# Ranks of messages pinned in three parts, and the first part of x loaded and normed first, in a two-layer graph kernel

## The chip, the cores and the metric

The kernel runs on one core of one Trainium2 chip. The metric is the device time of one execution in microseconds (us): the median of several runs, and beside it one execution that was taken with the hardware profiler, from which all durations below come. The engines are named as the profile names them: PE (matmuls), PEld (its weight loads), DVE (VectorE), ACT (ScalarE), POOL (GpSimd) and SP, which here only issues DMAs and loads registers. "DVE L807" is an instruction of VectorE that line 807 of the kernel before has issued.

## The reference

Two graph layers over 6250 nodes with 128 features and 106250 edges (100000 random ones in both directions, and a loop at each node), sorted by destination.

```python
edge_index = jnp.stack([src, dst])
h = jnp.maximum(_layernorm(x, axis=-1), 0.0)
x = x + layer0(h, edge_index, edge_type, ...)       # attention, 4 relations, 8 heads
h = jnp.maximum(_layernorm(x, axis=-1), 0.0)
x = x + layer1(h, edge_attr, src, dst, ...)         # messages both ways along each edge
```

Layer 0 projects the nodes once for each of four relations, takes a softmax of leaky logits over the edges that enter a node, for each relation and head, sums the weighted rows of the sources, and mixes the relations with a second small attention. Layer 1 computes `leaky_relu([nf[src], nf[dst], ef] @ We1) @ We2` for each edge in both directions, sums it at the node where it ends, and updates the node. So in layer 1 each edge gives one message to its destination and another to its source; the destinations are sorted, the sources are not.

## The kernel before

**Preparation** (lines 198 to 436). The nodes are cut into 50 units of 126 (`NU`, two blocks of 63, one in each half of the partitions). The weights come by ACT's DMA queue. The edge lists `src`, `dst`, the types `et` and the shifted `nxt` come by SP's queue as tiles of 128 x 832; then all of `x`, in five parts of ten units, each part as four DMAs (lines 242 to 252; the first two parts by ACT's queue, behind the weights, the rest by SP's). From the lists VectorE makes small tables that go to DRAM: `e2` (table row and destination of each edge), `turnd` (where a run of equal destinations begins or goes on, six writes), `lacks` (for each relation, the edges not of it, four writes from tiles `ne` of two buffers) and `dtyp` (lines 278 to 297), all on SP's queue. It also finds where each block's edges start (lines 301 to 345, into `st0`). SP then reads those starts into registers, ten at a time (line 165), and issues for each of the 100 blocks a load of its `e2` rows into `ct` (lines 350 to 358). Ten functions `columns` (line 364) turn `ct` into index columns `xi` and `dloc`; they stand in front of the last ten units.

The loop over units (lines 376 to 404) norms ten units at a time (`layernorm_relu`, line 141, into `h_sb` of two buffers), transposes a unit (PE L384), copies it (ACT, `hT`), multiplies it by the weights (PE L391, L394), copies the result to `row` (DVE L392) and `so` (ACT L398), both of three buffers, and stores them: `own` by ACT's queue (L400), the gather table `xt` by POOL's (L403). The DMAs of SP's and ACT's queues signal through eight semaphores that are handed out in turn over both queues; a DMA waits until the one that had its semaphore before has landed. The order of instructions on each engine comes from a scheduler, except where `tc.keep_in_program_order` pins an instruction; an engine then executes its instructions strictly in that order.

**Layer 0** (lines 441 to 891) goes in 25 steps `s` of four blocks, each of nine tiles `i` of 4 x 128 edges. POOL gathers the rows of `xt`, four gathers a tile (line 85, called in `gather0`), 17 tiles ahead, into 18 buffers `xg`. Each step, VectorE, ScalarE and PE do the messages of step `s` (line 604) and beside them the softmax of step `s + 1`: `logits` (line 530), four running scans in both directions (L571, L574, L581, L584) with a piece before an exponential (L577) and one behind a logarithm (L588), and `turn` (line 592), which leaves the weights `pw`. A dictionary `todo` says at which tile, and at which half of it, each of these pieces is issued: (i, 0) in the middle of the tile's four blocks, (i, 1) behind them. The nodes of step `s - 1` are finished in the same step (line 646).

**Ranks.** Layer 1 writes each message for a source to a place of its own. The place is a rank: how many edges before this one, in the same fifth of the partitions, go to a source of the same unit. Units are taken in 25 pairs. For each pair `count` (line 738) counts them, one VectorE instruction; `counted` (line 745) turns the counts into starting places in step 4; `rank` (line 802) then takes three instructions on the whole list of 128 x 832, for each pair:

```python
stt(own_, skey, float(g), sunit, op0=ALU.is_equal, op1=ALU.mult)
scan(place, own_, own_, base1[:, g:g + 1], op0=ALU.add, op1=ALU.max)
nc.vector.copy_predicated(plc, own_.bitcast(I32), place)
```

`own_` and `place` have one buffer each, and all operands lie in SBUF (`sunit` is bf16). `rank_at` (line 825) issues them behind tile 0 of steps 4, 5, ..., and also behind tile 5 of odd steps. They are not pinned. Behind the last pair `ranked` (line 810) makes the places whole, eight more instructions and one store, `plcd`, that layer 1 reads.

**Layer 1** (lines 945 to 1147) again gathers (900 times) and also scatters (900 times) with POOL.

Of the kernel before, what the change touches and what calls it, by code (L numbers as in the profile page):

```python
# [9 lines left out]
F32 = mybir.dt.float32  # L10
BF16 = mybir.dt.bfloat16
I32 = mybir.dt.int32
U8 = mybir.dt.uint8
AF = mybir.ActivationFunctionType
ALU = mybir.AluOpType
# [6 lines left out]
P = 128  # L22
# [4 lines left out]
R = 4  # L27
H, D = 8, 16
C = H * D
# [5 lines left out]
J = 832  # L35
JL = E - (P - 1) * J
JE = P * J
# [5 lines left out]
GB = 63  # L43
DB = 2 * GB
NU = -(-N // DB)
# [6 lines left out]
NS = NBK // Q  # L52
XR = C + H
SX = 2 * C + 2 * H
NEAR = 2.0 ** 100
# [3 lines left out]
NCS = 4  # L59
# [30 lines left out]
def kernel(ctx: ExitStack, tc: tile.TileContext, x, src, dst, ef, et, w_rel, a_src, a_dst,  # L90
# [10 lines left out]
    nc = tc.nc  # L101
# [96 lines left out]
    with ExitStack() as prep:  # L198
# [4 lines left out]

        wall = cpool.tile([P, R * XR + R * H + C + 2 * H], F32, name="wall")
# [24 lines left out]
        ints = {}  # L229
# [11 lines left out]

        x_sb = cpool.tile([P, NU, C], F32, name="x_sb")
        for u0 in range(0, NU, 10):
            nc.gpsimd.memset(x_sb[:, u0:u0 + 10, :], 0.0)
            for q in range(2):
                n0 = u0 * DB + q * GB
                k = 10 if u0 + 10 < NU else 9
                xq = x[u0 * DB:(u0 + k) * DB, :].rearrange("(u q r) c -> q r u c", q=2, r=GB)[q]
                for r0, r1 in ((0, 48), (48, GB)):
                    (nc.scalar if u0 < 20 else nc.sync).dma_start(x_sb[q * 64 + r0:q * 64 + r1, u0:u0 + k, :], xq[r0:r1])  # L250
        for h, n in halves(NU - 1):
            nc.sync.dma_start(x_sb[h, NU - 1, :], x[n, :])

# [30 lines left out]
        dn = cpool.tile([P, 2, J], BF16, name="dn")  # L284
        tt(dn[:, 1, :], ints["dst"], nxt, op=ALU.is_equal)
        ts_(dn[:, 0, :], dn[:, 1, :], -1.0, NEAR, op0=ALU.add, op1=ALU.mult)
        for k in range(2):
            nc.sync.dma_start(turnd[k, 1:JE + 1].rearrange("(p j) -> p j", j=J), dn[:, k, :])
            for o, w in ((0, 1), (JE + 1, 7)):
                nc.sync.dma_start(turnd[k:k + 1, o:o + w], dn[0:1, k, 0:w])  # L290
        for r in range(R):
            ne = wpool.tile([P, J], BF16, name="ne")
            ts_(ne, ints["et"], float(r), None, op0=ALU.not_equal)
            nc.sync.dma_start(lacks[r].rearrange("(p j) -> p j", j=J), ne)
        dty = cpool.tile([P, J], F32, name="dty")
        stt(dty, dstf, float(R), ints["et"], op0=ALU.mult, op1=ALU.add)
        nc.sync.dma_start(dtyp[0].rearrange("(p j) -> p j", j=J), dty)

# [61 lines left out]

        first = cpool.tile([P, NBK, TB], F32, name="first")
# [14 lines left out]
        for u in range(NU):  # L376
            if u >= NU - NBK // CG:
                columns(u - NU + NBK // CG)
            if u % 10 == 0:
                h_sb = wpool.tile([P, 10, C], F32, name="h_sb")  # L380
                sq = wpool.tile([P, 10, C], F32, name="sq", bufs=1)
                layernorm_relu(wpool, h_sb, x_sb[:, u:u + 10, :], sq)
            tp = pp.tile([P, P], F32, name="tp")
            nc.tensor.transpose(tp, h_sb[:, u % 10, :], ident)  # L384
            hT = wpool.tile([P, P], F32, name="hT")
            nc.scalar.copy(hT, tp)
            row = wpool.tile([P, R * XR], F32, name="row", bufs=3)
# [9 lines left out]
            so = wpool.tile([P, SX], F32, name="so", bufs=3)  # L397
# [43 lines left out]
    with ExitStack() as s1_:  # L441
# [360 lines left out]
        def rank(g):  # L802

            own_ = wp.tile([P, J], F32, name="own_", bufs=1)
            stt(own_, skey, float(g), sunit, op0=ALU.is_equal, op1=ALU.mult)
            place = wp.tile([P, J], F32, name="place", bufs=1)
            scan(place, own_, own_, base1[:, g:g + 1], op0=ALU.add, op1=ALU.max)  # L807
            nc.vector.copy_predicated(plc, own_.bitcast(I32), place)
# [16 lines left out]
        rank_at = [(s, i) for s in range(NCS, NS) for i in ((0, 5) if s % 2 else (0,))]  # L825
# [24 lines left out]
        for s in range(NS):  # L850
# [5 lines left out]
            if more:  # L856
                work(s + 1)
                for at, f in zip(((2, 0), (3, 1), (4, 0), (4, 1), (5, 0), (5, 1), (6, 0), (7, 0), (8, 0)), soft(s + 1)):
                    todo[at] = f
                for c in range(3):  # L860
                    todo[c, 1] = lambda c=c: logits(s + 1, c)
                gts.append(wp.tile([P, 2, R + 1], F32, name="gt", bufs=3))
            for i in range(TB):
                n = s * TB + i
                if n + LA0 < NS * TB:
                    gather0(n + LA0)
                messages(s, i, acc, turns_, todo.get((i, 0), lambda: None))
                todo.get((i, 1), lambda: None)()
                if more and i <= R:
                    tallies(s + 1, i, gts[s + 1])  # L870

                g = NC0 + s * TB + i
                if g < NU // 2:
                    count(g, True)
                if (s, i) == (NCS, 0):
                    counted()
                if (s, i) in rank_at[:NU // 2]:
                    rank(rank_at.index((s, i)))
                    if rank_at.index((s, i)) == NU // 2 - 1:
                        ranked()  # L880
                if i == 5 and s + 2 < NS:
                    loads(s + 2)
# [840 lines left out]
```

## Time and profile before

| | us |
|---|---|
| median of 3 runs (4106.76 to 4119.22) | 4111.01 |
| the profiled execution | 4104.87 |
| its span, first to last instruction | 4103.1 |
| busy: PE / DVE / ACT / POOL | 3053 / 2739 / 1545 / 2892 |
| first transposes of a unit (PE L384) | 42.9 |
| last load of `ct` issued (SP L356) | 146.4 |
| first gather (POOL L85) | 158.7 |
| last gather of layer 0 | 1402.3 |
| end of the last GELU of layer 0 (ACT L631) | 1468.2 |

A step of layer 0 is measured here from the end of its predecessor's eighth GELU (L631) to the end of its own. The steps, in us:

| step | 1 | 2 | 3 | 4 | 5 | 6 | 7 | 8 | 9 | 10 | 11 | 12 |
|---|---|---|---|---|---|---|---|---|---|---|---|---|
| length | 47.8 | 47.6 | 51.6 | 48.6 | 59.5 | 54.1 | 54.8 | 53.5 | 55.8 | 51.6 | 52.2 | 47.3 |
| in ranks (DVE) | 1.0 | 0 | 0 | 7.1 | 11.7 | 12.5 | 15.3 | 14.2 | 16.1 | 13.7 | 12.5 | 3.1 |

Steps 13 to 23 take 46.4 to 49.3 each and hold no rank. The three instructions of a rank take 1.02, 1.95 and 1.09; the first scan of a rank starts at 447.1, the last copy at 835.2.

How to read the profile's lines: a group line has the source line, engine, operation, output and input tiles, the count, then the busy time and the mean of one in ns, then the idle time of the engine just before, with what ended it. A timeline line has the start, the duration, engine, line and operation, and in brackets the idle time before it. A line of the windows view has the window, its length, and for PE, PEld, DVE, ACT and POOL the busy time with the number of instructions; then the granted clock of PE, the DMA share and GB/s. A line of the wait table has who waited for whom, the total in us, the times, and the longest. A busy sum of an engine does not say that it is the bottleneck: that is read from what ends the waits in a stage.

### The profile page before, as it was taken

Reading aid. Unit: us, or ns where it says so; the run is one execution under the profiler, and the core shown is the slowest. Engines: PE = TensorE matmul, PEld = TensorE weight load, DVE = VectorE, ACT = ScalarE, POOL = GpSimd, SP = SyncE. Lnnn points to the kernel's source line nnn. Section 1 sums busy time; section 2 is a strip of 40 time slices with the busy share of each in tenths; the row PEclk is TensorE's granted clock in tenths of the full one; section 3 lists DMA queues with packets and bytes.
Section 4 is the critical chain, followed back from the end, with each engine's and each line's share of the span. In section 5 each row is a group of like instructions: output and inputs, shape, how many; then the busy total and the mean of one; then the engine's idle time right before and its main releaser. Section 6 shows DMA issues by size and latency. Waiting matters only on the chain. (4 is left out here: it accounts for less than half of the span.)

```text
span 4103.1 us, 43438 instructions
## 1 busy us (share of the span) xinstructions
PE 3053.0 (74%) x11258; PEld 1729.4 (42%) x11258; DVE 2738.6 (67%) x5139; ACT 1545.1 (38%) x2990; POOL 2892.2 (70%) x2887
## 2 busy tenths in 40 slices
PE   4468877778887756666678877778768777688888
PEld 3346555555555532222234342334324333244455
DVE  7467888887777745555466665666657666577755
ACT  3256655566666622222223333222222322222211
POOL 5777787777777527777777777777777777777600
PEclk9669978899999978888899898999989998899999
DMA  7544444455555356666587886888868878588754
GB/s 193 160 101 122 115 114 115 116 123 121 122 129 127 92 135 186 178 178 182 164 252 236 254 249 183 246 245 242 248 198 259 246 234 248 174 260 272 228 167 140
DMA packets 414557, 754.19 MB, mean 184 GB/s; under 512 B 182846, under 2 KB 249380, under 8 KB 414300
## 3 DMA queue, kind: packets, MB, share of 16 engines
q0 software_dynamic: 148800, 430.91, 35.8%
q1 hardware_dynamic: 234314, 290.32, 27.2%
q10 hardware_dynamic: 31186, 30.10, 2.6%
q8 instruction: 92, 1.51, 0.2%
q14 instruction: 165, 1.35, 0.1%
HBM read 586.37 MB, written 164.69 MB: 183 GB/s over the span
## 5 line engine op out<-in xcount | busy, mean ns | idle before, releaser
L85 POOL DMA_INDIRECT xg<-xt,xi x900 | 970.8, 1079 | 274.4 <-issue 224.6
L1113 POOL DMA_INDIRECT m2d<-s,placei x900 | 913.1, 1015 | 294.6 <-issue 211.4
L85 POOL DMA_INDIRECT ag<-abtab,srci x900 | 907.7, 1009 | 294.6 <-issue 205.4
L1105 PE MATMUL z<-rhs,lt 128*128 128x512 f32 x1800 | 1032.5, 701 | 0.6 <-ACT lt L1069 0.6
L1109 DVE TENSOR_TENSOR s<-s,z 128x1024 f32<-128x1024 f32 x450 | 548.1, 1220 | 549.1 <-ACT z L1108 547.7
L1125 PE MATMUL sums<-s,oh 128*64 128x256 f32 x1800 | 335.2, 455 | 491.3 <-DVE s L1109 490.6
L1107 DVE TENSOR_TENSOR s<-z,ag 128x1024 f32<-128x1024 f32 x450 | 549.8, 1222 | 198.8 <-PE z L1105 154.3
L617 PE MATMUL acc<-oh,msg 128*128 128x256 f32 x1800 | 534.3, 435 | 174.2 <-DVE oh L616 168.9
L1108 ACT ACTIVATE z<-s 128x1024 f32<-128x1024 f32 x450 | 461.1, 1025 | 414.8 <-DVE s L1107 413.5
L1105 PEld LDWEIGHTS z<-rhs,lt 128*128 128x128 f32 x1800 | 352.5, 216 | 447.9 <-issue 441.0
L1016 PE MATMUL sums<-mt,ohw 128*128 128x256 f32 x2024 | 523.3, 392 | 8.7 <-DVE ohw L1015 8.7
L1110 ACT COPY s<-srcf 128x2 f32<-128x2 f32 x450 | 86.7, 193 | 1175.8 <-DMA m2d<-s,placei 1159.9
L617 PEld LDWEIGHTS acc<-oh,msg 128*128 128x128 f32 x1800 | 365.2, 216 | 279.7 <-DVE oh L616 210.3
L1016 PEld LDWEIGHTS sums<-mt,ohw 128*128 128x128 f32 x2024 | 389.3, 198 | 198.0 <-issue 128.5
L1125 PEld LDWEIGHTS sums<-s,oh 128*64 128x64 f32 x1800 | 98.6, 149 | 727.6 <-DVE s L1109 579.4
L616 DVE TENSOR_SCALAR oh<-iota,key 128x256 f32<-128x256 f32 x900 | 307.6, 363 | 144.0 <-PE acc L617 136.0
L624 ACT ACTIVATE junk<-dt,nthr 128x1152 bf16<-128x1152 f32 x250 | 312.9, 1252 | 0.2
L1015 DVE TENSOR_SCALAR ohw<-col,at 128x128 f32<-128x128 f32 x1012 | 250.1, 302 | 15.6 <-PE sums L1016 7.9
L1069 ACT COPY lt<-tp 64x384 f32<-64x384 f32 x300 | 141.7, 472 | 108.0 <-PE tp L1065 55.8
L1065 PE MATMUL tp<-ident,fe 128*128 128x128 f32 x450 | 83.6, 292 | 125.5 <-ACT lt L1069 95.6
L607 DVE TENSOR_TENSOR msg<-xg,pw 128x512 f32<-128x512 f32 x225 | 150.8, 684 | 14.6 <-ACT pw L602 14.4
L542 ACT COPY es<-xg 128x128 f32<-128x128 f32 x225 | 62.1, 297 | 221.1 <-DMA xg<-xt,xi 175.8
(417 smaller groups left out, 3227.3 us busy)
## 6 DMA issues: line engine op xcount, KB each, us to landing
mt<-m2d SPq DMA_DIRECT2D x156, 514.0 KB
db<-in_dst_dram SPq DMA_DIRECT2D x200, 288.0 KB
mt<-m2d SPq DMA_DIRECT2D x53, 642.5 KB
dt<-dtyp SPq DMA_DIRECT2D x100, 288.0 KB
fe<-in_edge_attr_dram SPq DMA_DIRECT2D x100, 288.0 KB
mt<-m2d SPq DMA_DIRECT2D x41, 385.5 KB
xg<-xt,xi POOLq DMA_INDIRECT x900
ag<-abtab,srci POOLq DMA_INDIRECT x900
```

What stands on the lines that cost most here:

```text
L85: nc.gpsimd.indirect_dma_start(out=o, out_offset=None, in_=table, in_offset=bass.IndirectOffsetOnAxis(ap=idx.bitcast(I32), axis=0))
L616: ts_(oh.rearrange("p t n -> p (t n)"), iota, key[:, k:k + 1], None, op0=ALU.is_equal)
L617: nc.tensor.matmul(acc[q // 2][:, :, q % 2, :], msg[:, q, :], oh, start=(i == 0 and q % 2 == 0), stop=(i == TB - 1), skip_group_check=True)
L624: nc.scalar.activation(junk, lanes[s]["dt"][v], AF.Sign, bias=nthr[:, u, t:t + 1], accum_out=g[:, v, t:t + 1])
L1015: ts_(oh, col, at[:, i:i + 1], None, op0=ALU.is_equal)
L1016: nc.tensor.matmul(sums, oh, mt[:, i, 0:HID], start=(i == 0), stop=(i == n - 1))
L1105: nc.tensor.matmul(z[:, q, :], lt[q][:, i * P:(i + 1) * P], rhs[(2 * u + q) % 4], start=True, stop=True)
L1107: tt(s[:, :, 0:2 * HID], z, ags.pop(n), op=ALU.add)
L1108: nc.scalar.mul(z, s[:, :, 0:2 * HID], 0.01)
L1109: tt(s[:, :, 0:2 * HID], s[:, :, 0:2 * HID], z, op=ALU.max)
L1113: st = nc.gpsimd.indirect_dma_start(out=m2d, out_offset=bass.IndirectOffsetOnAxis(ap=placei[:, k:k + 1], axis=0), in_=s[:, q, HID:HID + MW ...
L1125: nc.tensor.matmul(sums[q * 64:(q + 1) * 64, :], oh[:, q * TB + i, :], s[:, q, 0:HID], start=(i == 0), stop=(i == TB - 1))
```

## The change

Two things are changed.

First, the ranks. `rank` now returns its three instructions, and each is issued and pinned at its own half tile: the first pair of a step at (0, 0), (1, 0) and (2, 1), the second pair, in odd steps alone, at (7, 1), (8, 0) and (8, 1). The pairs go to the same steps in the program as before, 4 to 20; now their place on VectorE is theirs.

Second, the preparation. The loads of the first ten units of `x` are issued ahead of most weights on ACT's queue; the first four units are normed by themselves, early, the next six in front of the first unit, and each following ten seven units ahead, in a ring of 20. `row` and `so` get six buffers, `hT` three. The making of `turnd`, `lacks` and `dtyp` and their eleven writes move behind the loads of `ct`, where the writes are pinned on SP's queue.

```diff
+        x_sb = cpool.tile([P, NU, C], F32, name="x_sb")
+        def load_x(u0, queue):
+            nc.gpsimd.memset(x_sb[:, u0:u0 + 10, :], 0.0)
...
+                    queue.dma_start(x_sb[q * 64 + r0:q * 64 + r1, u0:u0 + k, :], xq[r0:r1])
+
+        def norm(u0, n):
+            sq = wpool.tile([P, 10, C], F32, name="sq", bufs=1)
+            layernorm_relu(wpool, h_sb[:, u0 % 20:u0 % 20 + n, :], x_sb[:, u0:u0 + n, :], sq[:, 0:n, :])
+
+        h_sb = cpool.tile([P, 20, C], F32, name="h_sb")
+        load_x(0, nc.scalar)
...
-        x_sb = cpool.tile([P, NU, C], F32, name="x_sb")
-        for u0 in range(0, NU, 10):
...
+        load_x(10, nc.scalar)
+        for u0 in range(20, NU, 10):
+            load_x(u0, nc.sync)
...
+        norm(0, 4)
...
-        dn = cpool.tile([P, 2, J], BF16, name="dn")
...
-        nc.sync.dma_start(dtyp[0].rearrange("(p j) -> p j", j=J), dty)
...
             cts.append(ct)
...
+        dn = cpool.tile([P, 2, J], BF16, name="dn")
...
+        c = nc.sync.dma_start(dtyp[0].rearrange("(p j) -> p j", j=J), dty)
+        tc.keep_in_program_order(c)
...
-            if u % 10 == 0:
-                h_sb = wpool.tile([P, 10, C], F32, name="h_sb")
-                sq = wpool.tile([P, 10, C], F32, name="sq", bufs=1)
-                layernorm_relu(wpool, h_sb, x_sb[:, u:u + 10, :], sq)
+            if u == 0:
+                norm(4, 6)
+            if u % 10 == 3 and u + 7 < NU:
+                norm(u + 7, 10)
...
-            hT = wpool.tile([P, P], F32, name="hT")
+            hT = wpool.tile([P, P], F32, name="hT", bufs=3)
...
-            row = wpool.tile([P, R * XR], F32, name="row", bufs=3)
+            row = wpool.tile([P, R * XR], F32, name="row", bufs=6)
...
-            so = wpool.tile([P, SX], F32, name="so", bufs=3)
+            so = wpool.tile([P, SX], F32, name="so", bufs=6)
...
-            stt(own_, skey, float(g), sunit, op0=ALU.is_equal, op1=ALU.mult)
             place = wp.tile([P, J], F32, name="place", bufs=1)
-            scan(place, own_, own_, base1[:, g:g + 1], op0=ALU.add, op1=ALU.max)
-            nc.vector.copy_predicated(plc, own_.bitcast(I32), place)
+            return [lambda: stt(own_, skey, float(g), sunit, op0=ALU.is_equal, op1=ALU.mult),
+                    lambda: scan(place, own_, own_, base1[:, g:g + 1], op0=ALU.add, op1=ALU.max),
+                    lambda: nc.vector.copy_predicated(plc, own_.bitcast(I32), place)]
...
-        rank_at = [(s, i) for s in range(NCS, NS) for i in ((0, 5) if s % 2 else (0,))]
+        rank_at = [(s, at) for s in range(NCS, NS) for at in (((0, 0), (1, 0), (2, 1)), ((7, 1), (8, 0), (8, 1)))[:1 + s % 2]]
...
+            pairs = [(g, at) for g, (t, at) in enumerate(rank_at[:NU // 2]) if t == s]
+            ranks = {}
+            def half(i, h):
+                f = todo.get((i, h))
+                if f:
+                    f()
+                for g, at in pairs:
+                    if (i, h) == at[0]:
+                        ranks[g] = rank(g)
+                    if (i, h) in at:
+                        tc.keep_in_program_order(ranks[g][at.index((i, h))]())
+                    if (i, h) == at[2] and g == NU // 2 - 1:
+                        ranked()
...
-                messages(s, i, acc, turns_, todo.get((i, 0), lambda: None))
-                todo.get((i, 1), lambda: None)()
+                messages(s, i, acc, turns_, lambda: half(i, 0))
+                half(i, 1)
```

## The prediction

> **What bounds the kernel now.** I read the page first (busy shares, the costliest groups), then the windows view cut at the steps of layer 0, then the timelines of GpSimd and VectorE beside each other, then the timelines and the wait table of the first 160 us. The chain of waits ends in the last store and tells nothing here.
>
> The page's costliest group is the gather of layer 0: 900 instructions on GpSimd, one behind the other, with only issue gaps between them.
>
> ```profile
> L85 POOL DMA_INDIRECT xg<-xt,xi x900 | 970.8, 1079 | 274.4 <-issue 224.6
> ```
>
> An undisturbed gather takes 0.95 us and the next one starts 0.30 us later, so 36 gathers, one step, need 45.2 us. A step (from the last GELU of L631 of one step to that of the next) takes 46.5 to 49 us where no rank runs. Layer 0 is bound by GpSimd. The windows view over six steps with 20 ranks and their closing instructions (steps 6 to 11) and six steps without (13 to 18); columns are PE, PEld, DVE, ACT, POOL:
>
> ```profile
> 550.60:872.70 322.10, 243.12 (x1045) 169.30 (x1044) 286.01 (x555) 189.73 (x356) 256.24 (x217) 0.85 0.48 113
> 920.00:1205.20 285.20, 234.00 (x1040) 164.80 (x1038) 218.47 (x494) 188.56 (x355) 219.68 (x216) 0.92 0.53 126
> ```
>
> The reader is to see that the first six steps are 36.9 us longer and that POOL is busy 36.5 us longer with the same gathers. VectorE still idles 36 us there. So ranks cost time through longer gathers, not through a full VectorE: 36.9 / 20 = 1.85 us a pair. The timelines show how:
>
> ```profile
> 657.56 1.95 DVE L807 TENSOR_TENSOR_SCAN place<-own__6835,base 128x832 f32<-128x832 f32 x1
> 657.65 2.62 POOL L85 DMA_INDIRECT xg<-xt,xi  x1 [0.30 <-issue]
> ...
> 987.78 2.56 DVE L574 TENSOR_TENSOR_SCAN a<-km,f 128x1152 f32<-128x1152 f32 x1
> 988.06 0.95 POOL L85 DMA_INDIRECT xg<-xt,xi  x1 [0.30 <-DVE f L571]
> ```
>
> A gather that starts 0.09 us into a rank scan (both inputs in SBUF) ends 0.76 us after that scan; one that starts in a softmax scan (one input in PSUM) is not touched. A gather that started before the rank instruction is not touched either: the hold is decided at the gather's start.
>
> The other part is the preparation, until the first gather:
>
> ```profile
> 42.92 0.69 PE L384 MATMUL tp<-ident,h_sb 128*128 128x128 f32 x2 [6.92 <-DVE h_sb L156]
> ...
> 62.77 83.93 SPq L356 DMA_DIRECT2D ct<-e  x100
> ...
> 149.50 0.29 DVE L367 CAST ctf<-ct 90x256 f32<-90x256 int32 x1 [4.78 <-DMA abtab<-zr]
> ...
> 158.66 1.40 POOL L85 DMA_INDIRECT xg<-xt,xi  x1 [0.46 <-DMA t<-turnd]
> ```
>
> The first transposes wait for the norm until 42.9; the 50 units follow; the hundred column loads on SP run in step with the units (they share eight completion semaphores with the `own` stores, and the wait table has SP waiting for those stores) and end at 146.7; the last columns and the last unit follow them, then the gathers. As gathers run without a pause from here to 1402, what is won here is won at the end.
>
> **Part 1, the ranks.** Nothing is removed: 25 times 1.02 + 1.95 + 1.09 us (rows of L805, L807, L808) stay, 101 us. They move from steps 4 to 11, up to four pairs a step, to steps 4 to 20, one or two a step. VectorE is busy 36.4 us of 47.6 in a step without ranks; with 4.1 or 8.1 more it still idles 3 us or more, so VectorE itself does not become the bound. What matters is the price at GpSimd. From both sides, by the rows: a gather under the first part took 0.95 to 2.11 us (0 to 1.16 more), one under the scan 1.43 to 2.75 (0.5 to 1.8), one under the copy 0.95 to 1.98 (0 to 1.0): 0.5 to 4.0 us a pair, 12 to 100 us for 25, against 46 now. For parts that stand alone and meet the gathers at any phase I work out the middle: a start in the first L - 0.19 us of a part waits for the rest, starts come every 1.26 us, so 0.83²/2/1.26 = 0.27 and 0.90²/2/1.26 = 0.32 for the two short parts, and 1.95 - 0.63 - 0.19 = 1.13 for the scan. 1.72 a pair, 43 for 25. I take this, which is nearest to the measured 1.85: -3 us. The relief that fewer ranks in a step seem to offer is paid out again over more steps. What waits behind a pinned part on VectorE: the second pair's first part stands in front of the sum of logarithms (old L588), so the weights come 1 us later in eight steps. From a step's last gather to its weights `pw` 40 us pass (877.1 to 917.7 for step 13); the first gather that needs a tile so freed starts at 925.8, which leaves some 5 us after the first `msg`. So that 1 us is hidden; without this cover it would cost 8 us in all.
>
> The Trainium skill, page "SBUF — State Buffer", section "Who interferes with whom", says that a VectorE instruction with two SBUF inputs contends with a GpSimd instruction that reads SBUF, and that the one that comes second blocks fully; it speaks against this change, since a lock is not eased by spreading its holders. The same section infers that descriptor generation needs only the write interface, by which two-input instructions would not hold these gathers at all and the ranks would cost them nothing before or after; the 2.62 us above says otherwise.
>
> **Part 2, the first part of x and its norm.** The four loads of units 0 to 9 go ahead of the small weights on ACT's queue, and a norm of four units is made first. In the changed program's order VectorE runs, from the arrival of `src` (7 to 9.5 us), priced by the distance of starts in the timeline of before: source units and `dstf` 8.1; reduces and subtract of the first units, at 0.4 and 0.6 of 1.46 each, 2.1; weight scores 3.8; `node`, `nthr` 0.8; `e2t`, `ends`, `holds`, `fall`, `dn`, one `ne` 5.9; `less`, count, second `ne` and the rest of the norm 3.7. 24.4 in all, so the first units are normed at about 33 instead of 42.9: 10 us earlier. The x loads have some 7 us until their reduce; the weights, now four issues later, have 8 us.
>
> **Part 3, pace of the units.** First to 47th `own` store: 47.35 to 141.52, 2.05 us a unit. Deeper `row`, `so` and `hT` take these waits away, and norms asked for seven units ahead those for `h_sb`:
>
> ```profile
> ACT so L398 <- DMA own<-so: 24.5, 28, 2.1
> DVE row L392 <- DMA xt<-row: 12.5, 11, 2.0
> ```
>
> They overlap, so not 37 us go. Next late are: VectorE at first (14 `row` copies at 0.68 and 20.6 us of norms and preparation stand among the first 14 units: 2.15 a unit), then PE and SP: units 36 to 43 took 1.80 each with PE full, and ten column loads take SP 4.6 plus a register load of 1.6 to 4.9 for every 4.3 units, 1.7 a unit or more. I take 1.85 (1.75 to 2.05). The first store stands 4.4 us after the first transposes as before, 37; then 14 x 2.15 = 30 and 31 x 1.85 = 57: the 46th store at 124.5, after which the last column loads may go.
>
> **Part 4, the tail, and what SP moves.** Eleven writes (six of `turnd`, four of `lacks`, `dtyp`) go behind the hundred column loads. Before: store 46 at 141.5, last load 4.9 later, first gather 12.3 after that. I keep both: 129.4, then 141.7. Beside the 12.3 now stands a chain of the moved writes, for the first gather waits for all `lacks`: six issues 2.1, `lacks` 0 to land 3.3 (issued 54.58, its reader went on at 57.9), a third `ne` that waits in VectorE's queue for that, 0.5, and another write, 0.8 + 3.3: 10 to 11 us. It hides behind the last unit by 1 to 2 us; if that cover is gone, each us is a us at the end, and the key instructions and counts queued behind `ne` on VectorE go with it. First gather at 141.7 instead of 158.7: -17 us (136 to 149: -23 to -10).
>
> **Sum.** -17 - 3 = -20. The profiled execution took 4104.87 us (span 4103.1), so 4085 on its scale. The median of the runs shown, 4111.01, lies 6 above it; against that I forecast 4091.
>
> **Rivals.**
> 1. VectorE was the bound of the crowded steps, and spreading hides the ranks: steps 4 to 12 fall to 47.6, some 46 us go beside the 17: 4048. For it: VectorE is busy 89% there, and step 4, with 7.1 us of rank, took only 48.6. Against it: POOL's own busy time holds the whole excess. 11%.
> 2. The preparation gives little: units stay at 2.05, or the chain of moved writes is late, first gather near 152, -7, ranks -3: 4101, within the bound. For it: column loads and stores stay in step. 19%.
> 3. Slower: the parts stand at fixed places in the tile, as the gathers do (four a tile), so the phase can be the same bad one in every step. If each part holds a fresh gather from its start, a pair costs 3.4 (0.8 + 1.75 + 0.9), 25 x 1.55 = 39 more: 4133. It turns the sign from 2.5 us a pair, and shows as a loss from 3.0. Old L588 shows such locking: most of its calls hold a gather to 1.73 us, old L577 to 1.2. 8%.
> 4. The pins don't hold, or the ranks stay crowded: -17 alone, 4094, inside the forecast's own range. The changed order has them in place.
>
> **Numbers.** Forecast 62%, 4076 to 4098. A measurement can tell about 0.3%, 12 us, from no change. Faster by more: forecast and rival 1, 0.72; within: rival 2 and a little of the rest, 0.20; slower: 0.08. The range leaves out rivals 1 and 3: 4060 is a first gather at 136 with 0.73 us a pair, 4110 one at 149 with 2.2; the outer bounds of 0.5 and 4.0 need the same extreme in all 75 parts.
>
> **What would show it.** First gather at 136 to 149; first transposes near 33; waits for `own` and `xt` nearly gone. Steps 4 to 20 each 2 to 4 us longer than steps 21 to 23, steps 6 to 11 some 49 to 51; POOL's time in gathers still near 971. If it falls to 930, rival 1 is right; at 1000 rival 3. A first gather past 150 breaks parts 3 or 4.

## The result and the profile after

The changed kernel takes 4116.65 us (median of 20 runs), the kernel before 4111.01 (20 runs): ratio 1.0017, 95% interval 1.001 to 1.0025. It is slower by 5.6 us, where 4091 was forecast, 20 below. The profiled execution took 4116.76 (span 4115.0), 11.9 more than that of before. By stage:

| us | before | changed | difference |
|---|---|---|---|
| until the first gather | 158.7 | 150.5 | -8.2 |
| first to last gather of layer 0 | 1243.7 | 1256.8 | +13.1 |
| last gather to the end of the last GELU | 65.9 | 66.4 | +0.5 |
| from there to the end | 2634.9 | 2641.4 | +6.5 |

The last row holds code that the change does not touch; in the kernels run on chips like this one (e3 aside) it lies between 2635 and 2652, so its 6.5 are the spread of single profiles. The first three give +5.4, the median's loss. The first row should have been -17, the second -3.

The group line of the gathers (busy, mean ns, idle before):

```profile
L85 POOL DMA_INDIRECT xg<-xt,xi x900 | 983.7, 1093 | 274.6 <-issue 224.9
```

The gathers themselves take 12.9 us more, with the same idle time: layer 0 is still one gather behind the other, and each is a little longer. The windows view over steps 6 to 11, 13 to 18 and 21 to 23 (PE, PEld, DVE, ACT, POOL):

```profile
538.90:848.00 309.10, 243.12 (x1038) 170.80 (x1039) 243.26 (x514) 188.73 (x354) 243.71 (x215) 0.88 0.50 118
898.40:1201.80 303.40, 246.45 (x1037) 173.46 (x1038) 246.81 (x520) 188.82 (x355) 237.27 (x218) 0.86 0.50 119
1307.90:1448.40 140.50, 116.14 (x509) 82.97 (x509) 107.15 (x244) 92.42 (x173) 77.67 (x76) 0.89 0.39 94
```

The ranks are spread as planned: steps 6 to 11 take 13.0 us less than before, steps 13 to 18, now with nine pairs, 18.2 more; steps 21 to 23, without ranks, take 46.8 each. (The last window also holds the time behind the last gather, so its POOL sum is short.) The relief is paid out again, and more than that.

One pinned pair in the timeline of VectorE and GpSimd (here and below, lines of other instructions in between are left out):

```profile
1194.03 1.06 DVE L824 SCALAR_TENSOR_TENSOR own__9884<-skey,sunit 128x832 f32<-128x832 f32 x1
1194.03 0.95 POOL L85 DMA_INDIRECT xg<-xt,xi  x1 [0.30 <-issue]
...
1200.90 1.94 DVE L825 TENSOR_TENSOR_SCAN place<-own__9884,base 128x832 f32<-128x832 f32 x1
1201.58 2.10 POOL L85 DMA_INDIRECT xg<-xt,xi  x1 [0.30 <-issue]
...
1212.07 1.09 DVE L826 COPY_PREDICATED plc<-own__9884,place 128x832 f32<-128x832 int32 x1
```

The parts stand 7 and 11 us apart. The first part holds none here (that gather began with it), and the scan holds one: 2.10 us, ending 0.84 after the scan. Now two pairs of the kernel before, where the scheduler was free (same view):

```profile
713.52 1.94 DVE L807 TENSOR_TENSOR_SCAN place<-own__7839,base 128x832 f32<-128x832 f32 x1
714.13 2.09 POOL L85 DMA_INDIRECT xg<-xt,xi  x1 [0.30 <-issue]
715.62 1.10 DVE L808 COPY_PREDICATED plc<-own__7839,place 128x832 f32<-128x832 int32 x1
716.53 0.98 POOL L85 DMA_INDIRECT xg<-xt,xi  x1 [0.30 <-issue]
717.13 1.02 DVE L805 SCALAR_TENSOR_TENSOR own__8250<-skey,sunit 128x832 f32<-128x832 f32 x1
717.81 1.16 POOL L85 DMA_INDIRECT xg<-xt,xi  x1 [0.30 <-issue]
```

The copy follows the scan within 0.2 us. The gather that the scan held ends at 716.22; the next one starts 0.31 later, when the copy has 0.19 us left, and takes 0.98. So the copy is all but free: it ran in the shelter of a gather that was held anyway. Counted in the traces, 42 of the 75 parts before began within 1.3 us of the end of the part ahead, after the change 9. Before, no gather started at all within 13 of the 25 first parts; after, within 3.

The preparation. The first transposes stand at 34.3 (33 expected), the first store at 38.7 (37). Then ScalarE in the last ten units, with the matmul on PE that waits for it (after the change):

```profile
119.27 0.37 ACT L414 COPY edbd<-po 64x32 f32<-64x32 f32 x2 [1.57 <-PE po L412]
119.66 0.28 ACT L416 COPY so<-po 128x144 f32<-128x144 f32 x1
119.84 0.27 ACT L404 COPY hT<-tp 128x128 f32<-128x128 f32 x1
120.16 1.18 PE L409 MATMUL ps<-wall,hT 128*128 128x272 f32 x4 [0.67 <-ACT hT L404]
```

`hT` of the next unit stands behind `edbd` and `so` of this one, so each unit runs through PE and ScalarE in turn: 2.40 us. The same stretch before:

```profile
121.60 0.27 ACT L386 COPY hT<-tp 128x128 f32<-128x128 f32 x1
...
122.37 0.28 ACT L398 COPY so<-po 128x144 f32<-128x144 f32 x1 [0.50 <-DMA own<-so]
...
123.34 0.27 ACT L386 COPY hT<-tp 128x128 f32<-128x128 f32 x1 [0.42 <-PE ps L391]
```

Here `hT` goes ahead of `so` of the unit before: 1.74 us. And the end of the preparation after the change:

```profile
142.92 0.33 ACTq L418 DMA_DIRECT2D own<-so  x1
...
144.31 1.09 DVE L370 TENSOR_SCALAR ne<-et 128x832 bf16<-128x832 int32 x2
144.92 0.83 SPq L371 DMA_DIRECT2D lacks<-ne  x2
...
145.81 0.45 SPq L375 DMA_DIRECT2D dtyp<-dty  x1
...
148.62 0.35 POOL L466 IOTA iota<- 128x256 f32 x1 [4.62 <-DMA dtyp<-dty]
...
150.50 1.05 POOL L85 DMA_INDIRECT xg<-xt,xi  x1 [0.72 <-issue]
```

The last unit is stored at 142.9; GpSimd then waits 4.6 us for the last of the moved writes. Before, the first gather came 4.1 us after the last store, now 7.6.

### The profile page after: what moved, and what is told of

It is laid out like the page before. It is cut to its first block, busy times and chain, and to the rows that moved or that the text cites. A ratio compares the mean times of both kernels' runs of the same rounds, so it can differ in the third digit from the quotient of the medians.

```text
span 4115.0 us, 43395 instructions
## 1 busy us (share of the span) xinstructions
PE 3073.2 (75%) x11258; PEld 1748.5 (42%) x11258; DVE 2733.9 (66%) x5145; ACT 1545.8 (38%) x2992; POOL 2912.2 (71%) x2887
## 3 DMA queue, kind: packets, MB, share of 16 engines
q14 instruction: 164, 1.34, 0.1%
## 5 line engine op out<-in xcount | busy, mean ns | idle before, releaser
L85 POOL DMA_INDIRECT xg<-xt,xi x900 | 983.7, 1093 | 274.6 <-issue 224.9
L85 POOL DMA_INDIRECT ag<-abtab,srci x900 | 915.9, 1018 | 292.5 <-issue 202.5
L1046 PE MATMUL sums<-mt,ohw 128*128 128x256 f32 x2024 | 521.8, 391 | 10.5 <-DVE ohw L1045 10.5
L635 PEld LDWEIGHTS acc<-oh,msg 128*128 128x128 f32 x1800 | 373.6, 220 | 252.5 <-DVE oh L634 179.3
L1095 PEld LDWEIGHTS tp<-ident,fe 128*128 128x128 f32 x450 | 57.8, 148 | 194.5 <-ACT lt L1099 130.3
```

The costliest lines, as they stand in the source:

```text
L85: nc.gpsimd.indirect_dma_start(out=o, out_offset=None, in_=table, in_offset=bass.IndirectOffsetOnAxis(ap=idx.bitcast(I32), axis=0))
L635: nc.tensor.matmul(acc[q // 2][:, :, q % 2, :], msg[:, q, :], oh, start=(i == 0 and q % 2 == 0), stop=(i == TB - 1), skip_group_check=True)
L1046: nc.tensor.matmul(sums, oh, mt[:, i, 0:HID], start=(i == 0), stop=(i == n - 1))
```

## The experiments

**Two theories.** A: the loss is in the ranks. A part holds a gather that starts in it; parts close together share one held gather, pinned ones half a tile apart each hold their own. P, for the preparation: the units gained no pace in the end because of ScalarE's order. Rivals: the earlier first gather shifted the gathers against all other VectorE instructions (B), the steps with ranks set the price and not the parts' distance (E), any long VectorE instruction holds gathers (D), column loads set the units' pace (F).

The runs fell on two kinds of chip. On the first (e1, e2, e3, e5, e13, e14) the kernel before took 4109 to 4111 us; on the other 4747 to 4791. There engines now and then waited without a cause that the profile shows, the gathers up to 23.6 us in e19. An expectation below says that all engines stopped for 4 to 20 us; the traces show less: in layer 0 of e19 all of them idle at once for 3.3 us at most (0.5 or less in the first profiles of both kernels), and the longer waits are those of one or several. Each ratio is against the kernel before on the same chip. Until the first gather the two kinds agree within the spread of the profiles, and for the preparation all runs are used.

### The two halves of the change: e1, e2

e1 is the kernel before with the diff of `rank`, `rank_at`, `half` and `messages`; e2 is the rest of the diff alone.

> The preparation of the kernel before, the ranks of the changed one. Theory A (the loss is in the ranks: a pinned part stands alone on VectorE and holds a gather of its own, where the parts before ran nearly back to back): first gather at 158.7 us as before, all gathers of L85 about 984 us of GpSimd, 1257 us from the first gather to the last, 4124 us in all, 13 above the kernel before. Rival B (the ranks cost the same wherever they stand; the earlier first gather shifted the gathers against VectorE's instructions, and that lengthened them): gathers 971 us, 1244 from first to last, 4111.

> The preparation of the changed kernel, the ranks of the kernel before (not pinned, up to four pairs a step). Theory A: first gather at 150.5 us, gathers 971 us, 1244 from first to last, 4103 us in all, 8 below the kernel before. Rival B: first gather at 150.5, gathers 984, 1257 from first to last, 4116.

e1: 4120.27 against 4111.2, ratio 1.0026 (1.0016 to 1.0036). e2: 4107.36, ratio 0.9993 (0.9982 to 1.0003). The ranks alone lose 9.1 us, the preparation alone gains 3.8, and together they make the 5.6. The single profiles are less tidy: 1247.5 us from first to last gather in e1, 1247.9 in e2, so both expected lengths were missed, by 9.5 and 3.9 us, and the gathers, 974.5 and 974.7 us, are equally long. (The profiled execution of e2 took 4117.77, 10 above its median.) What rank parts held can be counted in each trace (a gather whose end lies 0.76 us, give or take 0.15, behind that of a part; its time above 0.95), in us:

| | eq | scan | copy | sum | a pair |
|---|---|---|---|---|---|
| before | 4.3 | 24.2 | 8.4 | 36.8 | 1.47 |
| e2, old places | 2.4 | 21.9 | 7.7 | 32.0 | 1.28 |
| changed | 6.6 | 27.0 | 10.5 | 44.1 | 1.76 |
| e1, new places | 5.3 | 26.3 | 11.8 | 43.3 | 1.73 |
| e13, parts together | 6.4 | 24.2 | 2.9 | 33.5 | 1.34 |
| e5, scan with PSUM | 3.0 | 0.3 | 8.1 | 11.3 | 0.45 |

Old places 32 to 37, new places 43 to 44: 9.3 us between the means, as the medians have it (9.1, and 4116.65 - 4107.36 = 9.3). So B is not the cause of the loss: by B e1, with the first gather where it was, would lose nothing. A smaller effect of its kind stays possible. What gathers took above 0.95 us each and not under rank parts is 79.0 and 76.2 us with the old preparation (before, e1), 84.6 and 87.7 with the new one (changed, e2). Of the 12.9 us that the changed gathers take more, 7.3 lie under rank parts and 5.6 under other instructions, and no run separates these 5.6 from chance.

### No rank in the steps: e3

```diff
-                    if (i, h) in at:
-                        tc.keep_in_program_order(ranks[g][at.index((i, h))]())
...
+        for g in range(NU // 2):
+            for f in rank(g):
+                tc.keep_in_program_order(f())
+        ranked()
```

> The changed kernel with all 25 pairs of ranks and their closing instructions behind the last step of layer 0, where no gather of L85 runs; nothing is left out. The whole takes some 100 us longer; what counts is the time from the first gather to the last, 1257 us in the changed kernel and 1244 in the one before. Theory A, with the 44 us that I count in the trace under rank parts: about 1213. If pinned ranks also push other VectorE instructions into gathers: about 1198. If the ranks are not what makes the steps long (rival B, or a price under 1 us a pair): over 1232.

A single run took 4170.12 us, with 1210.7 from first to last gather, and on the page:

```profile
L85 POOL DMA_INDIRECT xg<-xt,xi x900 | 937.4, 1042 | 274.6 <-issue 219.1
```

Against it 25 pairs cost 33.0 us in the kernel before and 46.1 in the changed one, both within 4 us of the count above. With the profiles of e2 and e1, which have the same two placings, the differences are 37.2 and 36.8. So the term that failed is found: the price *before* was 33 to 37 us by both profiles and 32 to 37 by the count, and not 46. The pinned price is less sure, 37 to 46 by single profiles; that it is some 9 us above the old one rests on the medians and the count.

### What holds a gather: e5

```diff
-            pt = pe_.tile([P, 512], F32, name="pt")
+        weigh = pe_.tile([P, 512], F32, name="weigh")
+        nil = weigh[:, 511:512]
+        nc.vector.memset(nil, 0.0)
...
-                    lambda: scan(place, own_, own_, base1[:, g:g + 1], op0=ALU.add, op1=ALU.max),
+                    lambda: scan(place, own_, nil.to_broadcast([P, J]), base1[:, g:g + 1], op0=ALU.add, op1=ALU.max),
```

> The changed kernel, but the rank's scan takes a zero from PSUM as its second input in place of its own first input (same result, same length on VectorE, same order on VectorE, ScalarE and GpSimd). Theory A, with the hold tied to two inputs in SBUF: gathers under the scan are no longer held, 27 us of 984 go, 957 left, 4117 - 27 = 4090 us. Rival D (what holds a gather is a long VectorE instruction as such, or its writes): gathers 984, 4117 us.

The zero lies in the last column of the PSUM tile `weigh`. The edit also puts `pt` into that tile and takes it off the list of spare PSUM tiles for finishing nodes, in lines not shown.

4101.39 us, ratio 0.9975 (0.9966 to 0.9985), 15 below the changed kernel's median and 10 below the kernel before. The timeline of two scans:

```profile
542.25 1.94 DVE L827 TENSOR_TENSOR_SCAN place<-own__4506,base,weigh 128x832 f32<-128x832 f32 x1
542.94 0.95 POOL L85 DMA_INDIRECT xg<-xt,xi  x1 [0.30 <-issue]
...
884.09 1.93 DVE L827 TENSOR_TENSOR_SCAN place<-own__7391,base,weigh 128x832 f32<-128x832 f32 x1
884.09 0.95 POOL L85 DMA_INDIRECT xg<-xt,xi  x1 [0.30 <-issue]
885.35 0.95 POOL L85 DMA_INDIRECT xg<-xt,xi  x1 [0.30 <-issue]
```

Same length and same write. The gather at 542.94 starts 0.69 us into its scan and takes 0.95 us; the one at 1201.58 in the changed kernel started 0.68 into a scan and took 2.10. (The gather at 884.09 proves nothing, as it starts with its scan, but the next one passes too.) The scans' holds fall from 27.0 us to 0.3, one of 25. D is out. That the zero is also a single repeated element is not what matters by the softmax scan shown in the prediction (old L574): its PSUM input is as wide as its other one, and the gather under it took 0.95. The gathers as a whole fell by 20.9, not by the 27 expected: other instructions hold more (the `msg` product, old L607, 34.3 in place of 30.1). The Trainium skill, page "SBUF — State Buffer", section "Who interferes with whom", says that the second SBUF input of a VectorE instruction comes by a read interface that it shares with GpSimd, and that one with at most one SBUF input, outside the two-port modes, does not contend; the rows of the scans agree with it. One SBUF input is not always free here: in the changed kernel the mask `oT` of L541, with one tensor input, ran from 1299.59 to 1300.41, and the gather that started at 1299.75 took 1.49 us with no other VectorE instruction beside it. In which mode it ran no view shows.

### The parts of a pair together: e4, e9, e13

```diff
-        rank_at = [(s, at) for s in range(NCS, NS) for at in (((0, 0), (1, 0), (2, 1)), ((7, 1), (8, 0), (8, 1)))[:1 + s % 2]]
+        rank_at = [(s, at) for s in range(NCS, NS) for at in ((1, 0), (8, 0))[:1 + s % 2]]
...
+                    if (i, h) == at:
+                        for f in rank(g):
+                            tc.keep_in_program_order(f())
```

> The changed kernel with the same pairs in the same steps, but the three parts of a pair stand together on VectorE (at one place in the tile) in place of half a tile or a tile apart. Theory A (a part that follows one which held a gather ends before the next gather starts, so it holds none; the pins took that shelter away): 25 pairs cost about 33 us, as in the kernel before, not 46; gathers of L85 about 971 us, 1244 from the first to the last, 4117 - 13 = 4104 us. Rival E (the step or the number of steps with ranks sets the price, not the distance of the parts): gathers 984, 1257, 4117.

> The kernel of e4 once more (the three parts of a pair together on VectorE), since the chip of e4 left 0.7 us between two gathers in place of 0.3 and was not bound as the one before. Theory A: gathers of L85 about 971 us, 1244 from the first to the last, 4117 - 13 = 4104 us. Rival E (the step or the number of steps with ranks sets the price, not the distance of the parts): gathers 984, 1257, 4117.

> The kernel of e4 and e9 once more, in the hope of a chip like that of the first four runs (the chips of e4 to e12 stopped all engines for 4 to 20 us now and then, so that layer 0 was not bound by the gathers). Theory A: gathers of L85 about 971 us, 1244 from the first to the last, 4104 us. Rival E (the steps with ranks set the price, not the distance of a pair's parts): gathers 984, 1257, 4117.

e13, on the first kind of chip: 4095.92 against 4108.66, ratio 0.9968 (0.9957 to 0.9979); gathers 965.1 us, 1238.5 from first to last, 18 below the changed kernel with the same pairs in the same steps. A pair:

```profile
1128.99 1.02 DVE L824 SCALAR_TENSOR_TENSOR own__9420<-skey,sunit 128x832 f32<-128x832 f32 x1
1129.68 1.16 POOL L85 DMA_INDIRECT xg<-xt,xi  x1 [0.30 <-issue]
1130.19 1.94 DVE L825 TENSOR_TENSOR_SCAN place<-own__9420,base 128x832 f32<-128x832 f32 x1
1131.14 1.75 POOL L85 DMA_INDIRECT xg<-xt,xi  x1 [0.30 <-issue]
1132.29 1.09 DVE L826 COPY_PREDICATED plc<-own__9420,place 128x832 f32<-128x832 int32 x1
1133.20 1.01 POOL L85 DMA_INDIRECT xg<-xt,xi  x1 [0.30 <-issue]
```

Each part holds only the rest of its own length, and the copy all but passes between two gathers. E is out: with the pairs in the same steps the price falls, so distance matters. Of the 18 us the rank parts' own holds are 10.6 (44.1 to 33.5); 7.8 more lie under `msg` (30.1 to 22.3) and 6.2 under the mask of L541 (10.6 to 4.4), against small gains of others. Why these met fewer starts was not tried by itself. e4 and e9 (4786.57 against 4747.08, ratio 1.008, 1.0049 to 1.0112; 4827.03 against 4781.75, ratio 1.0083, 1.0054 to 1.0111) fell on the other kind of chip. The gathers got shorter there too (924.2 and 928.9 us against 945.0 and 947.8 in e8 and e19), but the idle time between them rose by 47 to 56, so the end came later.

### The preparation: e6, e7, e10, e11, e17

e6 asks for the next unit's transposes ahead, e7 takes the buffers back, e10 has four `ne`, e11 is e6 with e10, e17 puts the block of `dn`, `ne` and `dty` with its eleven writes back ahead of the column loads, unpinned. In turn (e7 also has `row` and `so` at three):

```diff
+            hT = ahead.pop(u) if u else turned(0)
+            if u + 1 < NU:
+                ahead[u + 1] = turned(u + 1)
...
-            hT = wpool.tile([P, P], F32, name="hT", bufs=3)
+            hT = wpool.tile([P, P], F32, name="hT")
...
-            ne = wpool.tile([P, J], BF16, name="ne")
+            ne = wpool.tile([P, J], BF16, name="ne", bufs=4)
```

> The changed kernel with the transposes of a unit of the preparation, and their copy by ScalarE (hT), asked for one unit ahead. Theory P (the units gained no pace because the copy to hT now stands on ScalarE behind edbd and so of the unit before, so that TensorE waits for it): the last ten units, 2.4 us each in the changed kernel, take 1.8; the 50th own store at 136 to 138 us in place of 141 to 144, first gather at 143 to 146, some 4111 us in all. Rival F (column loads on SP, or TensorE itself, set the pace): 50th store at 141 to 144, first gather at 149 to 151, 4117.

> The changed kernel with row, so and hT back at 3, 3 and 2 buffers. Theory P: the waits for own and xt come back in the first forty units, but ScalarE's order in the last ten is that of the kernel before (hT ahead), and these take 1.8 us each: 50th own store at 141 to 145, so the deeper buffers gained next to nothing. The prediction's part 3 (deeper buffers are worth 0.2 us a unit): 50th store at about 152, first gather at about 160.

> The changed kernel with four buffers for ne, so that no ne waits for a write of lacks to land. Theory Q (the first gather, 7.6 us after the last own store, waits for the writes moved behind the column loads: the third ne for the landing of lacks 0, dtyp behind it): first gather 4 to 5 us after the 50th own store, at 146 to 148 us, some 4114 in all. Rival (the last unit's stores set it anyway, as in the kernel before, where it was 4.2 us): 150 to 151, 4117.

> The transposes one unit ahead (as in e6) and four buffers for ne (as in e10). Theory P with Q: 50th own store at 134 to 137 us, first gather at 139 to 143, 4117 - 9 = 4108 us. If the moved writes are late for another reason than ne (their issue on SP, dtyp): first gather at 146 or later, 4113 or more.

> The changed kernel with the eleven writes of turnd, lacks and dtyp where the kernel before had them, ahead of the column loads; all else as changed. Theory W (what came last before the first gather was those moved writes, 3.5 us behind the last unit): 50th own store at 141 to 145 us, first gather 4 us after it, some 4113 us in all. Rival (the column loads, later by the writes, make the units later): 50th store at 147 or more, first gather at 151 or more, 4118.

All fell on the other kind of chip (e6 ratio 1.006, 1.0033 to 1.0086; e10 1.0072, 1.0048 to 1.0097; e11 1.0047, 1.0027 to 1.0067; e17 1.0066, 1.0039 to 1.0092; e7 a single run, 4800.38), so only times until the first gather are read:

| | first `row` | 10th | 40th | 49th | last `own` | first gather |
|---|---|---|---|---|---|---|
| before | 46.0 | 64.4 | 126.4 | 144.0 | 154.5 | 158.7 |
| changed | 38.6 | 57.9 | 114.2 | 135.8 | 142.9 | 150.5 |
| e6 | 38.9 | 55.0 | 108.4 | 124.3 | 134.1 | 147.4 |
| e7 | 39.0 | 58.1 | 118.0 | 134.4 | 144.9 | 152.8 |
| e10 | 39.9 | 57.4 | 113.7 | 135.4 | 139.5 | 147.4 |
| e11 | 39.8 | 56.2 | 109.0 | 124.0 | 134.8 | 144.1 |
| e17 | 42.9 | 62.4 | 121.3 | 142.4 | 151.4 | 155.4 |

For the spread: e2, e3, e4, e5, e8, e9, e13 and e19 have the changed preparation too. Over these nine profiles the last `own` lies between 139.1 and 145.0 and the first gather between 146.7 and 152.7, but the 40th to the 49th unit takes 21.7 us in every one, and the gather comes 7.6 to 7.8 us behind the last store. So the paces and this distance can be read to a few tenths of a us, the last two columns only to some 3.

P holds for the pace: from the 40th unit to the 49th the changed kernel takes 21.6 us, 2.40 a unit, e6 15.9, 1.77. F is out for that stretch. The first gather of e6, 147.4, was expected at 143 to 146 and lies within the spread: what the units gain is lost again behind them. e7 shows how the buffers undid themselves: with the old ones the first 40 units are 3.4 us slower, but without the free buffers the scheduler puts `hT` first again, and the last nine take 16.4. In all, e7 is 2 us later than the changed kernel, within the spread: deeper buffers were worth little, not 0.2 us in each unit.

At the tail my theory Q failed. With four `ne` the first gather is where I had it, at 147.4, but so it was in e2 with two (146.7), and it is still 7.9 us behind the last store (e10); with both edits (e11) 9.3. The eleven writes can only be issued behind the last column load, whatever `ne` does: in e14, which has both edits too, SP issues them from 133.6 to 138.6, GpSimd goes on at 141.7, and the first gather starts at 143.6. The more the units gain, the more this shows. That it would pay to undo the move was wrong too. e17 has its 4.0 us from store to gather, but starts later:

```profile
32.45 3.09 PE L330 MATMUL ps<-dstf,holds 128*100 128x416 f32 x4 [32.45 <-DVE holds L327]
...
39.57 0.33 PE L340 MATMUL tp<-ident,stc 100*1 100x100 f32 x1 [3.85 <-DVE stc L338]
...
39.69 0.42 PE L397 MATMUL tp<-ident,h_sb 128*128 128x128 f32 x1
```

The norm is done at 33.0 there, but PE's order has the counts of block starts ahead of the first unit, and on VectorE `dn`, `ne` and `dty` stand ahead of `holds`, from which these counts are made: the first transposes are 5.4 us later, the last store 8.5. So the move is worth some 8.5 us in front and costs 3.6 behind: more than half of what the preparation gained.

### Spread, and the versions that follow: e8, e19, e18, e12, e14, e15

> The changed kernel once more, for the spread of one profile against another: if the loss in the gathers is a property of the kernel, 1250 to 1262 us from the first gather to the last again (1244 in the kernel before) and the first gather at 148 to 152; if it is chance, 1244 or less is as likely.

> The changed kernel once more, for the same purpose: 1256.8 us from the first gather to the last in its first profile, 150.5 at the first gather. Within 3 us of both, the figures are the kernel's own; at 1250 half of the 13 us are chance.

> The kernel before once more, for the spread of one profile against another: 1243.7 us from the first gather to the last in the first profile. Within 3 us of it, the 13 us to the changed kernel are its own; if it lies near 1250, half of them are chance.

All three (4755.77, 4789.51, 4783.38) fell on the other kind of chip, so the spread of the gathers on the first kind stays open; the count under the rank parts, which agrees between the two kernels of each placing, stands in for it. (First to last gather there: 1582.0 and 1587.8 us for the changed kernel, 1573.3 for the one before, waits without a cause included.) First gather: 148.6 and 151.1 for the changed kernel, 153.6 for the one before, where it was 158.7 and, in e1, 156.2. The mean of the nine profiles with the changed preparation is 150.2, that of these three 156.2: a gain of 6 us, known to some 3. What the other kind of chip does, in the wait table of e19, 300 to 1200 us:

```profile
POOL xg L85 <- issue: 249.1, 459, 15.6
...
DVE oh L634 <- remote: 100.2, 24, 11.8
...
PEld lg L566 <- issue: 75.0, 10, 14.3
```

"issue" and "remote" are waits for which the profile shows no cause, up to 15.6 us; in the first profile the longest such wait of L85 is 0.3. VectorE's instructions are as long as on the first kind (`msg` 685 ns in both). The mean granted clock of PE is lower, 0.82 against 0.87 to 0.88. Whether that has to do with the waits, and what causes them, stays open.

e12 and e14 are e11 with the scan of e5; e15 is that with the parts together.

> e11 with the scan of e5 (a zero in PSUM as its second input). If the gains add: first gather at 139 to 143 us, gathers of L85 about 963 us, 4101 - 9 = 4092 us, below both kernels. If a shorter preparation shifts the gathers into other holds: gathers 970 or more, 4100.

> The kernel of e12 once more (transposes one unit ahead, four buffers for ne, a zero in PSUM as the scan's second input). If the gains add: first gather at 139 to 144 us, gathers of L85 about 963 us, 4093 us, below both kernels. If a shorter preparation shifts the gathers into other holds: gathers 970 or more, 4100.

> e14 with the three parts of a pair together, as in e13. If part of what e13 gave back is other VectorE instructions that no longer meet the start of a gather (msg, oT), it adds to the scan that no longer holds: under 1225 us from the first gather to the last (1232 in e14), about 4080 us. If together and PSUM save the same microseconds: 1232 or more, 4089.

e14, on the first kind of chip, is the best of all: 4088.62 against 4108.66, ratio 0.9951 (0.9937 to 0.9965), first gather at 143.6, and

```profile
L85 POOL DMA_INDIRECT xg<-xt,xi x900 | 958.4, 1065 | 273.9 <-issue 215.3
```

The gains add. But the same kernel on the other kind of chip (e12) takes 4833.93 against 4781.75, ratio 1.0107 (1.008 to 1.0134), and e15 4840.97 against 4791.15, 1.0113 (1.0084 to 1.0142). So it beats the kernel before only where the gathers bound layer 0; e15's question stays open.

## Why the prediction was wrong, point by point

**The bound** was right: layer 0 is bound by the gathers, ranks cost time by holding them, and VectorE is not the bound. **The price of pinned parts**, 1.72 us a pair, 43 for 25, was right by the count: 43 to 44 (37 to 46 by single profiles). In part that was luck, for it was worked out for gathers that meet a part at any phase, and the phases are locked: 18 of the 25 first parts meet a gather 0.01, 0.48 to 0.51 or 0.74 to 0.75 us after their start. **The price before failed.** "46 now" came from 36.9 / 20 out of the windows view. That difference is real, but not all of it is ranks: in those six steps the gathers took 49.1 us above 0.95 each, against 15.1 in the six without; by the count of the table rank parts held 27.4 of the 49.1, 1.37 a pair or 34 for 25, and of the other 21.7 some 5.5 lie under pieces of the second attention (`lgn` and `va`), 0 in the six steps without. The lines that I showed gave nearly the right rule, a hold decided near the gather's start, but I applied it to parts that stand alone and did not ask what it says of parts that follow one another: there it makes the second one cheap. With 33 to 37 in place of 46, 43 to 44 is no longer a gain of 3 but a loss of some 9, as the medians have it.

**The first units** were right: first normed units at 34.1 for 33, first store at 38.7 for 37. **Pace** was right for forty units: 2.14 us in the first ten (2.15), 1.88 from the 10th to the 40th (1.85). It failed in the last ten, 2.40 for 1.85, some 5 us: I asked which wait is next late and not whether the scheduler, with the wait gone, would order ScalarE otherwise, which the changed program's order shows. Another 1.9 us were an error of counting: 45 intervals were added up to a store that in the trace before is the 47th. **The tail**: the cover of 1 to 2 us over the moved writes was not there; they put the first gather 7.6 us behind the last store in place of 4.1. The column loads ended earlier in return, so 47th store to first gather took 16.7 (17.2 expected). First gather 150.5 for 141.7: 1.7 from the start, 1.9 from the count, some 5 from the last ten. And of the 6 to 8 us by which it came earlier only 3.8 are left in the median of e2; where the rest went was not found.

**Rivals.** The first (ranks hidden) is out: gathers 983.7, not 930. The second (the preparation gives little, first gather near 152) came nearest for its part, and by one of its two causes, the late writes. The third had the sign but not the size: the phase is locked indeed, but a pair costs 1.76, not 3.4. No rival had a present price below my own; that was the one needed. Of the marks set, steps 12 to 20 take 4.3 us more each than steps 21 to 23 where 2 to 4 were named, steps 6 to 11 take 51.5 where some 49 to 51 were, and a first gather past 150 did break part 3.

## What to carry to other kernels

Price what stands there now as carefully as what replaces it: leave it out or count it instruction by instruction, since a difference between two windows charges it with everything else that differs. Where instructions of one engine hold those of another at their start, put the holders close together, or take the second SBUF input away from them. After making buffers deeper, read the new order of each engine, since a scheduler that no longer sees a wait may put a late instruction first.

## What the runs showed of the hardware

For the scan, the hold hangs on where its second input lies: 25 scans of 1.95 us held 25 gathers for 27.0 us with both inputs in SBUF, and one for 0.3 with a broadcast zero from PSUM. It is not decided exactly at the gather's start, as I had put it: a gather that began 0.17 us ahead of a copy was held by it, while the one at 1194.03 above, which began with its part, took 0.95. The kernel before had such rows too: the gather of 2.11 us that the prediction counts under a first part began 0.18 ahead of it. Only gathers are seen to wait: the parts of VectorE keep their length (scans 1.93 to 1.96 in the changed kernel), also where they begin in a running gather.

```profile
1157.35 2.07 POOL L85 DMA_INDIRECT xg<-xt,xi  x1 [0.30 <-issue]
1157.52 1.11 DVE L826 COPY_PREDICATED plc<-own__9473,place 128x832 f32<-128x832 int32 x1
```

And one program took 4110 us on some chips and 4750 to 4790 on others, with VectorE instructions of the same length: which change paid depended on the chip.
